# Layer 0 of a two-layer kernel: which matrix products are cut into smaller ones

## The chip, the cores and the metric

The kernel runs on one core of a Trainium2 chip. The metric is the device time of one execution in microseconds (us); less is better. A core has five engines with a queue each: TensorE (PE) multiplies matrices, VectorE (DVE), ScalarE (ACT) and GpSimd (POOL) work on elements, and SyncE (SP) issues most of the transfers between the off-chip memory and the on-chip memory. PE reads its operands from on-chip memory and writes into PSUM, eight banks of 512 float32 columns on 128 partitions, from which the other engines take the results. In the profile a PE product shows as weight loads (PEld) and matmul records (PE).

## What is computed

Two images of 128 channels and 256 by 256 pixels pass through two layers, each with a group normalisation ahead and a residual addition behind. Layer 0 is a windowed attention: every window of 8 x 8 pixels has its queries, every enlarged window of 12 x 12 its keys and values, with four heads of 32 channels, a relative position term, and a mask that keeps only some of the pairs.

```python
qkv = einsum('bchw,oc->bohw', gn(x), W_qkv)
q, k, v = split(qkv, 3, axis=1)
q = windows_8x8(q) * SCALE;  k, v = windows_12x12(k), windows_12x12(v)
attn = einsum('bnd,bmd->bnm', q, k)
attn = attn + rel_pos_emb(q, rel_height, rel_width) + FIXED_MASK
attn = softmax(attn, axis=-1)
out = einsum('bnm,bmd->bnd', attn, v)
x = x + einsum('bchw,oc->bohw', out, W_out)          # layer 0

t1 = conv(gn(x), w1)                                  # 5 x 1
t3 = depthwise_conv(t1, w3)                           # 3 x 1
t4 = einsum('nckhw,ckg->nghw', unfold_w3_dil2(gn(x)), w4)
x = x + t4[:, None] * t3                              # layer 1
```

Everything is float32.

## The kernel before

The mask lets a pixel attend only to pixels of certain row and column parities, so layer 0 is sorted by parity. An image is cut into 32 strips of 8 rows, 64 strips for both (index `k`). A strip is worked off in two units, one for each row parity `r`; unit `u` is `2 * k + r`, and there are 128. Layer 1 follows, strip by strip; its first pieces are called in the last units.

The order of the work is written out by hand in the loop over the units, and each engine keeps to it. For PE a unit has these steps, in this order; the line is that of the matmul in the profile:

1. `biases(u)` (L593): the position coefficients times a constant of ones and zeros are added up in the four score banks `f_s`; 16 products of 32 rows, 64 weight columns and 256 moving columns.
2. `scores(u, split)` (L610): 64 products of keys and queries, added to the same banks. Weights are 64 keys on 64 rows, the moving operand 64 queries: `[2, 32]`, of which the first index is the head of a pair. They go in turn to four quarters of PE's array of 64 rows by 64 columns (`g` picks the rows, `c` the columns). The first `split` of them are made as two products of 32 columns each, with the same weights.
3. `keys(u + 1, cuts, cuts)` (L413, through `in_parts`): two banks `f_pk` of 512 columns, one for each column parity, with the 128 x 128 key weights. `cuts` gives the parts of a bank.
4. `coefficients(k + 1, r)` (L504): one bank `f_pa` with 16 products. The weights `wb` are 128 rows by 64 columns (the position vectors for one place in the window), the moving operand `xq` has 64 columns. `half` decides on which 64 of the bank's partitions, that is on which columns of PE's array, the product lands; the loop runs over eight places `t` and inside it over the two halves. ACT (L513) and DVE (L517) then copy the bank into `f_cf`, one after the other, for the biases of the next strip.
5. `attend(u)` (L636): 64 products of 32 weight columns with 66 moving columns, after ACT has taken the exponentials of the scores (L620, four instructions).
6. In even units `values(k + 1)` (L526), 16 products; in odd units `queries` for the next two units (L476 and L478), 24 products.
7. `project(u)` (L413 again, in the two banks `f_py`), after DVE has divided and transposed the attention's output; DVE adds the residual (L672) and SP stores the rows.

How often a product is cut is set by `pieces(u)`: the parts of a bank for keys, queries and projection, and as a fourth number the scores to be split. `ONE`, `TWO` and `THREE` are the cuts in sixteenths of a bank: `(0, 16)`, `(0, 8, 16)` and `(0, 6, 11, 16)`, so that three parts of a bank have 192, 160 and 160 columns and two have 256 each. Units 0, 1, 60, 62, 63, 64 and 70 have entries of their own in `PIECES`; all others take the default of L316. No values are changed by a cut: the same columns are multiplied, in more or fewer instructions.

A product of float32 operands appears in the trace as two matmul records and two weight loads. All PSUM banks other than the scores' come from one pool of four, taken in turn.

Of the kernel before, what the change touches and what calls it, by code (L numbers as in the profile page):

```python
# [28 lines left out]
ONE, TWO, THREE, FOUR = (0, 16), (0, 8, 16), (0, 6, 11, 16), (0, 4, 8, 12, 16)  # L29
NKEY = 60  # L30
PIECES = {
    0: (ONE, ONE, ONE, 0), 1: (ONE, ONE, THREE, 1),
    60: (THREE, TWO, THREE, 0), 62: (ONE, TWO, ONE, 1), 63: (THREE, TWO, THREE, 3), 64: (TWO, TWO, THREE, 1),
    70: (TWO, TWO, THREE, 1),
}
# [161 lines left out]
def attention_fast(tc, io, x1_d, norm, st_x, st_y, tags, ends, weights, both, layer1):  # L197

    nc = tc.nc
    x = io["x"]  # L200
# [3 lines left out]
    with ExitStack() as l0:  # L204
# [3 lines left out]
        def cload(name, src, shape, pool=cst):  # L208
# [20 lines left out]
        kt = [cst.tile([P, 2, NPAIR * NKEY + 4], F32, tag=f"f_kt{r}", name=f"f_kt{r}") for r in range(2)]  # L229
# [3 lines left out]
        sc = [  # L233
            [ps_s.tile([P, 8, 2, 32], F32, tag=f"s{2 * g + i}", name=f"f_s{g}{i}") for i in range(2)]
            for g in range(2)
        ]

        xq = both.sb.tile([P, 2, 4, 4, 2, 2, 8, 2], F32, tag="xq", name="f_xq")
        wb = both.sb.tile([P, 4, 4, HEADS, 16], F32, tag="wb", name="f_wb")
# [8 lines left out]
        raws, norms, qs, cfs, pts, ots, rcs, ons, x1s = ({} for _ in range(9))  # L248
# [11 lines left out]
        with ExitStack() as setup:  # L260
# [9 lines left out]
            for i in range(first):  # L270
                t = sp.tile([P, 8, W], F32, tag="sx", name=f"f_sx_0_{i}")
                for lo in range(0, 8, 8 if i else 4):
                    hi = lo + (8 if i else 4)
# [28 lines left out]
            for i in range(first, NS - 2):  # L302
                t = sp.tile([P, 8, W], F32, tag="sx", name=f"f_sx_0_{i}")
# [9 lines left out]

        def pieces(u):

            return PIECES.get(u, (THREE, TWO, THREE, 5 if u % 2 else 2 if u % 6 == 0 else 1))  # L316

# [2 lines left out]
        for b in range(NB - 1):  # L322
            row = 0
            for i in range(NS - 4):
                n = 10 if i < 16 else 8
# [20 lines left out]
        def input_stats(u):  # L346
            b, row, n = stats_at[u]
            norm.chunk(st_x[b], row // 2, sxs.pop(u))

        def slots_of(k):  # L350

            first = (4 * k + 2) % 6
            return [(0, 4, first)] if first < 4 else [(0, 2, 4), (2, 2, 0)]
# [135 lines left out]

            return [lambda c=c: part(c) for c in range(2)]  # L490

        def coefficients(k, r):

            if r == 0:
                cfs[k] = wk.tile([P, 2, 2, 2, 8, 2, 16], F32, tag="cf", name=f"f_cf_{k}")
            pa = ps_pj.tile([P, 512], F32, tag="pj", name=f"f_pa_{k}_{r}")  # L500
            for t in range(8):
                t2, t1 = 2 * r + t // 4, t % 4
                for half in range(2):
                    nc.tensor.matmul(  # L504
                        pa[64 * half : 64 * half + 64, 64 * t : 64 * t + 64],
                        wb[:, t2, t1].rearrange("p h x -> p (h x)"),
                        xq[:, half, t2, t1].rearrange("p r c n e -> p (r c n e)"), start=True, stop=True,
                    )
            src = pa.rearrange("p (t m e) -> p e m t", t=8, e=2)
            for i in range(2):  # L510
                dst = cfs[k][..., i, 8 * r : 8 * r + 8].rearrange("p e r c n t -> p e (r c n) t")
                if i == 0:
                    nc.scalar.activation(  # L513
                        dst, src, AF.Identity, bias=keep[:, 1:2], scale=keep[:, 0:1]
                    )
                else:
                    nc.vector.tensor_scalar(  # L517
                        dst, src, keep[:, 2:3], keep[:, 3:4], ALU.mult, ALU.add
                    )
# [79 lines left out]
                                start=e == 0, stop=False, skip_group_check=True,  # L599
                            )  # L600

        def scores(u, split):
            k, r = divmod(u, 2)
            done = 0
            for n in range(NPAIR):
                for g in range(2):
                    rows = slice(64 * g, 64 * g + 64)
                    for c in range(2):
                        for lo, hi in ((0, 1), (1, 2)) if done < split else ((0, 2),):
                            nc.tensor.matmul(  # L610
                                sc[g][n // 8][64 * c : 64 * c + 64, n % 8, lo:hi].rearrange("p i x -> p (i x)"),
                                kt[r][rows, c, NKEY * n : NKEY * n + 64],
                                qs[u][rows, c, n, lo:hi].rearrange("p i x -> p (i x)"),
                                start=False, stop=n % 8 == 7, skip_group_check=True,
                            )
                        done += 1
            pts[u] = wk.tile([P, 2, NPAIR, 2, 32], F32, tag="p", name=f"f_p_{u}", bufs=1)
            for half in range(2):
                for g in range(2):
                    seen["exp", half, g] = nc.scalar.activation(  # L620
                        pts[u][:, g, 8 * half : 8 * half + 8].rearrange("p n i x -> p (n i x)"),
                        sc[g][half].rearrange("p n i x -> p (n i x)"), AF.Exp,
                    )
# [62 lines left out]
        def step():  # L686
            if chains and next(chains[0], True):
                chains.pop()

        def emit(parts):  # L690
            for f in parts:
                f()

        weights.load()
        with tc.manual_schedule(engines=ORDERED):
            normalise(0)
            emit(keys(0, ONE, ONE))
            top_values(0)
            bring_top(0, 0)
            values(0, range(4))  # L700
            for r in range(2):
                bring(r, slots_of(0))
            by_place(0, (0, 4))
            coefficients(0, 0)
            coefficients(0, 1)
            normalise(1)
            by_place(1, (0, 2))
            for u in range(2):
                emit(queries(u, ONE, ONE))
            for u in range(NU):  # L710
                k, r = divmod(u, 2)
                b, s = divmod(k, NS)
                later, more = u + 1 < NU, k + 1 < NB * NS
                if r == 1 and k + 2 < NB * NS:
                    normalise(k + 2)
                if u in stats_at:
                    input_stats(u)
                if u in norm_at:
                    st, i, name = norm_at[u]
                    chains.append(norm.steps(st[i], ps_pj, name, last=False))  # L720
                if u == 8:
                    weights.sums()
                if u in (NU - 4, NU - 2, NU - 1):
                    next(layer1)
                biases(u)
                scores(u, pieces(u)[3])
                if r == 0:
                    if k + 2 < NB * NS:
                        load_rows(k + 2, seen["exp", 0, 0])
                    if s == 0:  # L730
                        bring_top(1, b)
                step()
                at_top = more and (k + 1) % NS == 0
                cuts = pieces(u)[0]
                if later:
                    emit(keys(u + 1, cuts, cuts))
                step()
                if more:
                    coefficients(k + 1, r)
                elif later:  # L740
                    next(layer1)
                if k % NS == NS - 2:
                    step()
                attend(u)
                if u == 2 or u in stats_at:
                    load_next()
                if more and r == 1:
                    bring(1, slots_of(k + 1))
                if not later:
                    next(layer1)  # L750
                turn(u)
                if k % NS == NS - 2:
                    step()
                if r == 0 and more:
                    if at_top:
                        top_values(b + 1)
                        bring_top(0, b + 1)
                    values(k + 1, range(4))
                    bring(0, slots_of(k + 1))
                elif later and more:  # L760
                    cuts = pieces(u)[1]
                    emit(queries(u + 1, cuts, cuts) + queries(u + 2, cuts, cuts))
                if more and r == 0:
                    by_place(k + 1, (2, 4))
                elif k + 2 < NB * NS:
                    by_place(k + 2, (0, 2))
                if u > 0:
                    result_stats(u - 1)
                project(u)
                if u in quarter_at:  # L770
                    st, i, name, part = quarter_at[u]
                    norm.quarter(st[i], name, part)
                del qs[u]
            result_stats(NU - 1)
# [968 lines left out]
```

## Time and profile before

| | |
|---|---|
| median of 3 runs | 2866.58 us (2865.91 to 2869.38) |
| the profiled execution | 2865.81 us, its span 2863.9 us |
| keys, L413 f_pk, records of 160 and 192 columns | 976 and 488, mean 299 and 352 ns |
| projection, L413 f_py, records of 160 and 192 columns | 1008 and 504, mean 299 and 327 ns |
| scores, L610, records of 64 and 32 columns | 15592 and 1584, mean 220 and 223 ns |
| coefficients, L504, records of 64 columns | 4096, mean 225 ns |
| attention, L636 | 16384, mean 220 ns |
| values, L526 | 2048, mean 278 ns |

A record's duration holds the time from its start to a modelled end, and records overlap: the next one has mostly started before one ends, and several run beside each other where they use different parts of the array. So the durations say little on cost; the distance between starts does. A step's cost is read as the time from its first record's start to the first start of the next step. Layer 0 is the stretch from about 113 us to about 1870 us of the span.

### The profile page before, as it was taken

The numbers are of one execution on the slowest core, as the hardware profiler recorded it, in microseconds if no ns is written. First come the engines' busy times: TensorE is split into PE (matmuls) and PEld (weight loads), VectorE is DVE, ScalarE is ACT, GpSimd is POOL, SyncE is SP. The second block draws the span as 40 slices with busy tenths as digits, with TensorE's granted clock in tenths as the row PEclk, the third lists the DMA queues.
The fourth block names the chain that finished last, engine by engine and source line by source line (L and its number), as shares of the span: only waits on it lengthen the run. The fifth ranks groups of instructions, "written<-read, shape, count | busy, mean of one in ns | idle before, by whom it ended". The sixth has DMA issues, their size and how long they took to land.

```text
span 2863.9 us, 117440 instructions
## 1 busy us (share of the span) xinstructions
PE 2749.8 (96%) x51762; PEld 2086.8 (73%) x51762; DVE 2133.8 (75%) x3601; ACT 1506.7 (53%) x2379; POOL 642.8 (22%) x2049
## 2 busy tenths in 40 slices
PE   0699999999999999999999999999999999999998
PEld 0499999999999898999999999854444444444444
DVE  8667777767777565666666666689999998999987
ACT  1345455454554545455454454556666656666654
POOL 1333333333333333333333333200000000000000
PEclk9999999999999999999999999999999999999999
DMA  9566666666666455555554455467888888888885
GB/s 397 169 194 175 193 187 177 195 177 176 184 163 172 120 149 148 129 139 136 146 142 129 140 140 141 122 178 211 225 213 216 218 219 206 221 222 211 216 217 149
DMA packets 157556, 519.74 MB, mean 181 GB/s; under 512 B 20752, under 2 KB 98032, under 8 KB 117232
## 3 DMA queue, kind: packets, MB, share of 16 engines
q1 hardware_dynamic: 147968, 446.07, 52.7%
q0 software_dynamic: 9072, 66.06, 12.4%
q8 instruction: 412, 6.75, 1.0%
q14 instruction: 104, 0.85, 0.1%
HBM read 282.68 MB, written 134.22 MB: 146 GB/s over the span
## 4 chain that ended last, share of the span: by engine, by line
PE 79%; issue 17%; DMA 1%; POOL 1%; ACT 1%; DVE 1%; SPq 0%; POOLq 0%; ACTq 0%; DVEq 0%
PE f_s L610 10%; PE f_o L636 9%; PE f_pk L413 8%; PE f_pv L526 8%; PE f_py L413 8%; PE a_o L923 6%; PE a_e L923 6%; PE f_pq L478 6%; PE f_pa L504 5%; PE f_s L593 5%; PE f_pq L476 2%; PE a_d L974 2%; PE a_c L923 1%; PE b L1016 1%; PE g L903 1%
## 5 line engine op out<-in xcount | busy, mean ns | idle before, releaser
L517 DVE TENSOR_SCALAR f_cf<-f_pa,f_keep 128x512 f32<-128x512 f32 x128 | 103.8, 811 | 539.7 <-ACT f_cf L513 539.6
L620 ACT ACTIVATE f_p<-f_s 128x512 f32<-128x512 f32 x512 | 264.4, 602 | 400.4 <-PE f_s L610 400.3
L484 ACT ACTIVATE f_q<-f_pq,f_head 128x512 f32<-128x512 f32 x512 | 303.4, 703 | 141.0 <-PE f_pq L478 140.9
L427 POOL COPY f_kt<-f_kt 128x60 f32<-128x60 f32 (+1 forms) x348 | 106.2, 341 | 1167.4 <-ACT f_kt L441 1143.7
L998 ACT ACTIVATE t<-t,w 128x1024 f32<-128x1024 f32 x127 | 145.8, 1148 | 367.5 <-DVE t L991 362.5
L404 POOL COPY f_xq<-f_xn 128x96 f32<-128x96 f32 x1024 | 334.3, 356 | 3.3 <-DVE f_xn L387 3.3
L1005 DVE SCALAR_TENSOR_TENSOR t<-t,w,t 128x1024 f32<-128x1024 f32 x254 | 326.0, 1283 | 7.3 <-ACT t L998 1.3
L610 PEld LDWEIGHTS f_s<-f_q,f_kt 64*64 64x64 f32 x17176 | 270.3, 132 | 49.2 <-issue 49.2
L610 PE MATMUL f_s<-f_q,f_kt 64*64 64x64 f32 (+1 forms) x17176 | 287.9, 220 | 0.0
L636 PE MATMUL f_o<-f_vt,f_p 128*32 128x66 f32 x16384 | 263.2, 220 | 1.9 <-issue 1.9
L1034 POOL DMA_DIRECT2D y<-f_x x63 | 54.7, 868 | 916.8 <-DVE y L1026 870.8
L413 PE MATMUL f_pk<-f_xn,f_wqkvT 128*128 128x192 f32 (+3 forms) x1496 | 257.6, 321 | 0.7 <-ACT f_kt L441 0.7
L636 PEld LDWEIGHTS f_o<-f_vt,f_p 128*32 128x32 f32 x16384 | 241.6, 108 | 11.2 <-issue 2.2
L526 PE MATMUL f_pv<-f_wqkvT,f_xn 128*128 128x128 f32 x2048 | 246.2, 278 | 0.8 <-DVE f_cf L517 0.3
L923 PE MATMUL a_o<-xm,w1s 128*128 128x512 f32 x512 | 242.1, 594 | 4.6 <-ACT t L914 4.6
L413 PE MATMUL f_py<-f_ot,f_woT 128*128 128x160 f32 (+1 forms) x1520 | 243.9, 310 | 2.1 <-DVE f_ot L656 1.8
L923 PE MATMUL a_e<-xm,w1s 128*128 128x512 f32 x512 | 240.7, 591 | 0.0
L526 PEld LDWEIGHTS f_pv<-f_wqkvT,f_xn 128*128 128x128 f32 x2048 | 233.8, 192 | 7.2 <-issue 0.8
L413 PEld LDWEIGHTS f_pk<-f_xn,f_wqkvT 128*128 128x128 f32 x1496 | 221.4, 190 | 12.5 <-issue 1.7
L413 PEld LDWEIGHTS f_py<-f_ot,f_woT 128*128 128x128 f32 x1520 | 227.4, 190 | 4.1 <-issue 3.3
L478 PE MATMUL f_pq<-f_xn,f_wq_s 128*128 128x192 f32 (+1 forms) x1008 | 208.9, 329 | 0.0
L645 DVE TENSOR_TENSOR f_on<-f_o,f_rc 128x320 f32<-128x320 f32 (+1 forms) x384 | 197.2, 514 | 13.3
(150 smaller groups left out, 4656.5 us busy)
## 6 DMA issues: line engine op xcount, KB each, us to landing
f_raw<-in_x SPq DMA_DIRECT2D x62, 1280.0 KB
f_x<-f_x SPq DMA_DIRECT2D x128, 512.0 KB
y<-f_x POOLq DMA_DIRECT2D x63, 1024.0 KB, 7.9
out<-y SPq DMA_DIRECT2D x63, 1024.0 KB
f_vt<-f_vn SPq DMA_DIRECT2D x172, 264.0 KB
f_sx<-in_x SPq DMA_DIRECT2D x41, 1024.0 KB
raw<-f_x SPq DMA_DIRECT2D x64, 640.0 KB
raw<-f_x SPq DMA_DIRECT2D x62, 384.0 KB
```

Source lines behind the costliest of these rows:

```text
L404: nc.gpsimd.tensor_copy(xq[:, half, t2, 1:4, :, c].rearrange("p t r n e -> p r t n e"), xn[k % 2][:, windows, :, c, 0:3, t2:8:4].rearrange ...
L413: nc.tensor.matmul(dst[:, 512 * lo // last : 512 * hi // last], w, moving[:, n * lo // last : n * hi // last], start=True, stop=True,)
L478: nc.tensor.matmul(by_pair[:, lo:hi, 8:32], wq_s, xn[k % 2][:, lo:hi, r, c, 0:3].rearrange("p n i j -> p n (i j)"), start=True, stop=True,)
L484: nc.scalar.activation(q[:, c, :, i].rearrange("p n (j t) -> p n j t", t=4), pq.rearrange("p (n t j) -> p n j t", n=NPAIR, t=4), AF.Copy, ...
L526: nc.tensor.matmul(pv[:, P * n : P * n + P], xn[k % 2][:, 4 * g + n].rearrange("p r c i j -> p (r c i j)"), wvT, start=True, stop=True,)
L610: nc.tensor.matmul(sc[g][n // 8][64 * c : 64 * c + 64, n % 8, lo:hi].rearrange("p i x -> p (i x)"), kt[r][rows, c, NKEY * n : NKEY * n + 6 ...
L620: seen["exp", half, g] = nc.scalar.activation(pts[u][:, g, 8 * half : 8 * half + 8].rearrange("p n i x -> p (n i x)"), sc[g][half].rearran ...
L636: nc.tensor.matmul(po[32 * h : 32 * h + 32, n - lo], p[:, h // 2, n, h % 2], vt[r][:, :, n, h], start=True, stop=True,)
L645: nc.vector.tensor_tensor(on[:, :, lo:hi].rearrange("p c n d -> p n c d"), po[:, :, :, 0:32], rc.to_broadcast([P, hi - lo, 2, 32]), ALU.mult,)
L923: nc.tensor.matmul(pa[:, : n * W], w, rows, start=i == 0, stop=i == len(terms) - 1)
L998: nc.scalar.activation(t3[:, j : j + 4], t1[:, j : j + 4, :], AF.Copy, scale=w3[:, 0:1])
L1005: nc.vector.scalar_tensor_tensor(t3[:, j : j + 4], t1[:, j + tap : j + tap + 4, :], w3[:, tap : tap + 1], t3[:, j : j + 4], ALU.mult, ALU.add,
```

## The change

The default of `pieces` cuts keys and projection into two parts a bank, and the fourth number is larger. `scores` loses its argument: all its products are whole. `coefficients` gets one: of the 16 products of its bank, the first `split` are made as two products of 32 moving columns, with the same weights each time. The loop hands it the fourth number of `pieces`. The table `PIECES` stays as it is, so its fourth numbers now count coefficient products too.

```diff
-            return PIECES.get(u, (THREE, TWO, THREE, 5 if u % 2 else 2 if u % 6 == 0 else 1))
+            return PIECES.get(u, (TWO, TWO, TWO, 9 if u % 2 else 6 if u % 6 == 0 else 5))
...
-        def coefficients(k, r):
+        def coefficients(k, r, split=0):
...
                 for half in range(2):
-                    nc.tensor.matmul(
-                        pa[64 * half : 64 * half + 64, 64 * t : 64 * t + 64],
-                        wb[:, t2, t1].rearrange("p h x -> p (h x)"),
-                        xq[:, half, t2, t1].rearrange("p r c n e -> p (r c n e)"), start=True, stop=True,
-                    )
+                    for lo, hi in ((0, 1), (1, 2)) if 2 * t + half < split else ((0, 2),):
+                        nc.tensor.matmul(
+                            pa[64 * half : 64 * half + 64, 64 * t + 32 * lo : 64 * t + 32 * hi],
+                            wb[:, t2, t1].rearrange("p h x -> p (h x)"),
+                            xq[:, half, t2, t1, lo:hi].rearrange("p r c n e -> p (r c n e)"),
+                            start=True, stop=True,
+                        )
...
-        def scores(u, split):
+        def scores(u):
             k, r = divmod(u, 2)
-            done = 0
...
-                        for lo, hi in ((0, 1), (1, 2)) if done < split else ((0, 2),):
-                            nc.tensor.matmul(
-                                sc[g][n // 8][64 * c : 64 * c + 64, n % 8, lo:hi].rearrange("p i x -> p (i x)"),
-                                kt[r][rows, c, NKEY * n : NKEY * n + 64],
-                                qs[u][rows, c, n, lo:hi].rearrange("p i x -> p (i x)"),
-                                start=False, stop=n % 8 == 7, skip_group_check=True,
-                            )
-                        done += 1
+                        nc.tensor.matmul(
+                            sc[g][n // 8][64 * c : 64 * c + 64, n % 8].rearrange("p i x -> p (i x)"),
+                            kt[r][rows, c, NKEY * n : NKEY * n + 64],
+                            qs[u][rows, c, n].rearrange("p i x -> p (i x)"),
+                            start=False, stop=n % 8 == 7, skip_group_check=True,
+                        )
...
-                scores(u, pieces(u)[3])
+                scores(u)
...
-                    coefficients(k + 1, r)
+                    coefficients(k + 1, r, pieces(u)[3])
```

## The prediction

> **What bounds the kernel now.** I read the busy shares first, then the waits of TensorE, then the stretch of layer 0 by engine, then two neighbouring units (one unit is half a strip of 8 rows) in order of time. The page's first part and the chain by engine and line:
>
> ```profile
> PE 2749.8 (96%) x51762; PEld 2086.8 (73%) x51762; DVE 2133.8 (75%) x3601; ACT 1506.7 (53%) x2379; POOL 642.8 (22%) x2049
> PE 79%; issue 17%; DMA 1%; POOL 1%; ACT 1%; DVE 1%; SPq 0%; POOLq 0%; ACTq 0%; DVEq 0%
> PE   0699999999999999999999999999999999999998
> PEclk9999999999999999999999999999999999999999
> ```
>
> TensorE (PE) is the bound on average, at full clock. The change touches layer 0 alone, so its own stretch counts. The stage table for two long stretches of it (columns: stretch, its length, then busy time and instructions of PE, its weight loads, DVE, ACT and POOL, clock, DMA share and rate):
>
> ```profile
> 200.00:939.00 739.00, 738.66 (x20385) 683.15 (x20375) 528.95 (x1078) 373.23 (x684) 241.54 (x826) 1.00 0.65 180
> 1110.00:1848.00 738.00, 737.45 (x20413) 681.22 (x20412) 449.07 (x945) 373.30 (x684) 235.08 (x809) 1.00 0.53 138
> ```
>
> PE is idle 0.3 us in 739, and the next engine, DVE, works 529. What lengthens or shortens PE's work here goes straight into the time. Units 50 (even) and 51 (odd) in order of time (start, length to the last end, line, operation, shape of the first, number of records):
>
> ```profile
> 802.01 1.12 PE L593 MATMUL f_s<-f_cf,f_hot 32*64 32x256 f32 x32
> 803.06 2.19 PE L610 MATMUL f_s<-f_q,f_kt 64*64 64x32 f32 x130
> 805.18 2.00 PE L413 MATMUL f_pk<-f_xn,f_wqkvT 128*128 128x192 f32 x12
> 807.12 1.15 PE L504 MATMUL f_pa<-f_xq,f_wb 128*64 128x64 f32 x32
> 808.20 2.05 PE L636 MATMUL f_o<-f_vt,f_p 128*32 128x66 f32 x128
> 810.18 3.84 PE L526 MATMUL f_pv<-f_wqkvT,f_xn 128*128 128x128 f32 x32
> 813.85 1.90 PE L413 MATMUL f_py<-f_ot,f_woT 128*128 128x192 f32 x12
> 815.68 1.12 PE L593 MATMUL f_s<-f_cf,f_hot 32*64 32x256 f32 x32
> 816.73 2.31 PE L610 MATMUL f_s<-f_q,f_kt 64*64 64x32 f32 x138
> 818.97 2.00 PE L413 MATMUL f_pk<-f_xn,f_wqkvT 128*128 128x192 f32 x12
> 820.90 1.15 PE L504 MATMUL f_pa<-f_xq,f_wb 128*64 128x64 f32 x32
> 821.99 2.05 PE L636 MATMUL f_o<-f_vt,f_p 128*32 128x66 f32 x128
> ```
>
> The reader is to subtract starts. A product is two records (128 for 64 whole score products, 32 for 16 coefficient products), and each split product adds two. A step costs from its start to the next one's: scores 2.12 us with one split (unit 50) and 2.24 with five (unit 51), keys 1.94, coefficients 1.08, projection 1.83. The same row with none, two and three splits, from units 60, 54 and 63, each with the step that follows it:
>
> ```profile
> 940.24 2.10 PE L610 MATMUL f_s<-f_q,f_kt 64*64 64x64 f32 x128
> 942.27 0.38 PE L161 MATMUL pv_x<-q_x,f_gavg 128*128 128x1 f32 x2
> ...
> 857.84 2.21 PE L610 MATMUL f_s<-f_q,f_kt 64*64 64x32 f32 x132
> 859.98 0.73 PE L413 MATMUL f_pk<-f_xn,f_wqkvT 128*128 128x192 f32 x3
> ...
> 983.81 2.22 PE L610 MATMUL f_s<-f_q,f_kt 64*64 64x32 f32 x134
> 985.96 1.13 PE L453 MATMUL f_pk_top<-f_top,f_wqkvT 128*128 128x256 f32 x4
> ```
>
> So 0, 1, 2, 3 and 5 splits cost 2.03, 2.12, 2.14, 2.15 and 2.24 us. The cost isn't linear: the first costs 0.09 to 0.10, the second and third 0.01 each, and the fifth brings it to 0.21. That is the key to the change. The score products go in turn to four 64x64 quarters of the array, which work beside each other. The first split puts one quarter behind by two records; the next three are in the other quarters and lie beside it; the fifth is again in the first. What counts is the number of splits in the fullest quarter: n of them cost about 117n - 20 ns.
>
> **What the skill says.** "TensorE: Matmul & The Clock Gate", section "LDWEIGHTS (loading the stationary operand)", gives a weight load as columns / 1.2 ns, whatever the rows: 53 ns for 64 columns. "TensorEngine Tiling (Array Packing)", "Key Properties", says that tiles load and multiply in parallel, and its "Instruction Overhead" warns that a matmul with few moving columns is no shorter than one with 60. The trace agrees: within a quarter, score records start 58 ns apart, for 64 moving columns as for 32. A 32-column record saves nothing, since the 64 columns of weights are loaded again for it: 2 x 58 = 117 ns, the slope found above. "Runtime: NRT & Kernel Launch", "Instruction fetch mechanics", says that instructions arrive in blocks of 256; the page's q8 row (412 packets, 6.75 MB, so 16 KB each) fits that. It bears on a rival below.
>
> **The change part by part.** By `pieces`, an odd unit now has nine split coefficient products where it had five split score products; an even one five (six in every sixth unit) where it had one (two). Keys and projection go from three parts a bank to two. The products of a unit stay 189 (190 in every sixth): -2 keys, -2 projection, -5 or -1 or -2 scores, +9 or +5 or +6 coefficients. With "k+1 exists" and the table PIECES, 61 odd units, 39 plain even and 19 sixth ones are concerned; units 0, 1, 60, 62, 63, 64 and 70 swap nothing or equal numbers.
>
> *Scores removed.* Odd 2.24 - 2.03 = 0.21 us; even 0.10; sixth 0.11.
>
> *Keys and projection.* Between records of 160, 192 and 256 columns the trace has 136, 162 and 216 ns. Three parts in two banks: 8 x 136 + 4 x 162 = 1736 ns; two parts: 8 x 216 = 1728. So 8 ns less for each, 16 a unit: next to nothing, since columns and not instructions set this cost. The keys' second record is 105 ns late after the switch from the scores (267 instead of 162); that switch stays.
>
> *Coefficients added.* They use two column halves of the array with 64 weight columns each, records again 58 ns apart in a half (16 x 58 = 0.93, with 0.15 of start the 1.08 seen). The splits go to t = 0, 1, ... and there to half 0, then half 1. Nine: five in half 0, four in half 1. Five: three and two. Six: three each. No row shows a 32-column coefficient product. From below it costs what its columns cost, half as much, so almost nothing; from above the two halves get in each other's way and each split takes 175 ns. I take the score's law, for the weights have the same 64 columns and the records the same 58 ns: 5 x 117 - 20 = 565 ns for nine, 3 x 117 - 20 = 331 for five, 337 for six (a few ns of later start).
>
> *Sum.* Odd: +565 - 213 - 16 = +336 ns, x61 = 20.5 us. Plain even: +331 - 97 - 16 = +218, x39 = 8.5. Sixth: +337 - 110 - 16 = +211, x19 = 4.0. Unit 63 (three splits, two in half 0): +0.1. Units 126 and 127 have no coefficients left to make and lose 0.35. Together +32.8 us. The profiled execution took 2865.81 us (span 2863.9), 0.8 below the median of 2866.58; on the median the sum is 2899.4. I forecast 2899.
>
> *What hides or follows.* Nothing hides it: PE is not waiting. What waits for the coefficients (ACT's and DVE's f_cf, L513 and L517, then DVE's reciprocals and transposes for the projection) runs from their end, and the attention and value or query products that cover it follow at the same distance. The exponentials on ACT (4 x 0.60 us after the scores) get more cover, not less. No DMA, SP or POOL instruction is moved and no wait is added. Layer 1 starts that much later and is as long as before.
>
> **Rivals.**
>
> *A 32-column coefficient record is bound by its columns.* Then the removed parts win: odd -229, even -113, sixth -126 ns, in all -20.8 us; with 5 ns for each added record in the fuller half (50 and 30 ns a unit) +4.8 us come back: 2851. For it speaks only that this shape isn't in the trace with all 128 rows; against it the 58 ns of the 32-column score records with the same weight width. It decides if a split costs less than 117n - 20 by about 60%. Chance 0.06.
>
> *The halves no longer run side by side.* Four records in one half before the other's first: 175 ns a split, +129 us, about 2996. The scores with five splits show quarters starting 13 ns apart and running together, so 0.03.
>
> *Block boundaries of the instruction stream.* A unit is 378 records with as many weight loads and some twelve waits, 768 instructions or three blocks, so a boundary keeps its place in the unit. Before the attention, the new order moves products against it by up to 28 instructions. If a boundary then opened a gap of the size of the exposed weight load (105 ns) in each unit, +12.5 us on top: 2912. No such gap is seen before. Chance 0.06.
>
> *The change doesn't reach the end*, as other engines were late anyway: the 0.3 us of idle in 739 leaves no room; 0.01 for about no change.
>
> **The numbers.** Forecast 0.84, column-bound 0.06, serial halves 0.03, boundaries 0.06, no effect 0.01. The forecast's own bounds: records 53 ns apart (the load alone) give +27, no saving at the start +37. Range 2892 to 2907: it leaves out the column-bound, serial and boundary cases, 0.15 together. A measurement of this kernel can tell a change from none above about 0.2%, 5.7 us. Faster 0.06, same 0.01, slower 0.93.
>
> **What will show it.** Scores at 2.03 us in all units; coefficients at 1.65 us (odd) and 1.41 (even); keys and projection shorter by 0.01 each; an odd unit 13.71 to 14.04, an even one 13.67 or 13.69 to about 13.90; f_pa's records 4096 to 5826, f_s at L610 from 17176 to 16384; the gap between records of a half 58 ns at 32 columns too. A coefficient step under 1.3 us in odd units would make the forecast wrong, and so would a new idle place of PE.

## The result and the profile after

The changed kernel takes 2900.49 us (median of 4 runs, 2897.63 to 2902.3) against 2867.24 for the kernel before: ratio 1.0113, 95% interval 1.0101 to 1.0125. It is 33 us slower, where 2899 us was forecast. Its profiled execution took 2902.3 us, with a span of 2900.4.

The page of the changed kernel, busy shares and chain, and the stage table for a stretch of layer 0 (columns as before):

```profile
PE 2785.0 (96%) x51736; PEld 2046.2 (71%) x51736; DVE 2132.9 (74%) x3601; ACT 1507.3 (52%) x2379; POOL 641.6 (22%) x2049
PE 80%; issue 17%; DMA 1%; POOL 1%; DVE 1%; ACT 0%; SPq 0%; POOLq 0%; DVEq 0%; ACTq 0%
```

```profile
200.00:950.00 750.00, 748.75 (x20293) 659.13 (x20296) 523.81 (x1066) 369.06 (x677) 238.19 (x816) 1.00 0.63 177
```

PE executes 26 records fewer than before and is busy 35 us longer. It is nearly as closely packed as it was (idle 1.3 us of these 750, where it was 0.3 of 739), so the time is in the records, not between them. One plain even unit and the odd one after it, in order of time:

```profile
818.15 2.10 PE L610 MATMUL f_s<-f_q,f_kt 64*64 64x64 f32 x128
820.17 2.00 PE L413 MATMUL f_pk<-f_xn,f_wqkvT 128*128 128x256 f32 x8
822.10 1.50 PE L505 MATMUL f_pa<-f_xq,f_wb 128*64 128x32 f32 x42
823.52 2.05 PE L635 MATMUL f_o<-f_vt,f_p 128*32 128x66 f32 x128
825.50 3.84 PE L528 MATMUL f_pv<-f_wqkvT,f_xn 128*128 128x128 f32 x32
829.17 1.89 PE L413 MATMUL f_py<-f_ot,f_woT 128*128 128x256 f32 x8
831.00 1.12 PE L595 MATMUL f_s<-f_cf,f_hot 32*64 32x256 f32 x32
832.04 2.10 PE L610 MATMUL f_s<-f_q,f_kt 64*64 64x64 f32 x128
834.07 1.99 PE L413 MATMUL f_pk<-f_xn,f_wqkvT 128*128 128x256 f32 x8
835.99 1.73 PE L505 MATMUL f_pa<-f_xq,f_wb 128*64 128x32 f32 x50
837.65 2.05 PE L635 MATMUL f_o<-f_vt,f_p 128*32 128x66 f32 x128
```

Start to start, the scores are down to 2.03 us in both, keys and projection are 1.93 and 1.83 (shorter by 0.01), and the coefficients went from 1.08 to 1.42 (five splits) and 1.66 us (nine). The typical (median) step over all units, from its start to the next step's start in nanoseconds (a sixth unit is an even one whose number six divides, a plain even one is any other):

| step | before | after | forecast of the difference | measured |
|---|---|---|---|---|
| scores, odd / plain even / sixth | 2238 / 2122 / 2135 | 2025 | -213 / -97 / -110 | -213 / -97 / -110 |
| keys and projection, each | 1934, 1830 | 1924, 1820 | -8 | -10 |
| coefficients, odd (nine splits) | 1082 | 1658 | +565 | +576 |
| coefficients, plain even (five) | 1082 | 1419 | +331 | +337 |
| coefficients, sixth (six) | 1082 | 1451 | +337 | +369 |

With 61, 39 and 19 units the measured column gives 20.9 + 8.6 + 4.5 us, with the special and last units 33.8. The medians differ by 33.25.

### The profile page after: what moved, and what is told of

It reads as the page before. It is cut to its first block, busy times and chain, and to the rows that moved or that the text cites. A ratio compares the mean times of both kernels' runs of the same rounds, so it can differ in the third digit from the quotient of the medians.

```text
span 2900.4 us, 117389 instructions
## 1 busy us (share of the span) xinstructions
PE 2785.0 (96%) x51736; PEld 2046.2 (71%) x51736; DVE 2132.9 (74%) x3601; ACT 1507.3 (52%) x2379; POOL 641.6 (22%) x2049
## 4 chain that ended last, share of the span: by engine, by line
PE 80%; issue 17%; DMA 1%; POOL 1%; DVE 1%; ACT 0%; SPq 0%; POOLq 0%; DVEq 0%; ACTq 0%
PE f_s L610 9%; PE f_o L635 9%; PE f_pk L413 9%; PE f_pv L528 8%; PE f_py L413 8%; PE f_pa L505 7%; PE a_o L922 6%; PE a_e L922 6%; PE f_pq L478 6%; PE f_s L595 5%; PE f_pq L476 2%; PE a_d L973 2%; PE a_c L922 1%; PE b L1015 1%; PE g L902 1%
## 5 line engine op out<-in xcount | busy, mean ns | idle before, releaser
L610 PEld LDWEIGHTS f_s<-f_q,f_kt 64*64 64x64 f32 x16384 | 250.7, 135 | 49.5 <-issue 49.5
L610 PE MATMUL f_s<-f_q,f_kt 64*64 64x64 f32 x16384 | 268.4, 220 | 0.2 <-issue 0.2
L413 PE MATMUL f_pk<-f_xn,f_wqkvT 128*128 128x256 f32 (+2 forms) x1016 | 256.5, 395 | 0.7 <-ACT f_kt L441 0.7
L413 PE MATMUL f_py<-f_ot,f_woT 128*128 128x256 f32 (+3 forms) x1036 | 242.4, 377 | 2.0 <-DVE f_ot L655 1.8
L505 PEld LDWEIGHTS f_pa<-f_xq,f_wb 128*64 128x64 f32 x5826 | 186.2, 137 | 44.5 <-issue 43.5
L505 PE MATMUL f_pa<-f_xq,f_wb 128*64 128x32 f32 (+1 forms) x5826 | 203.7, 225 | 1.5 <-ACT f_kt L441 0.8
```

Source lines behind the costliest of these rows:

```text
L413: nc.tensor.matmul(dst[:, 512 * lo // last : 512 * hi // last], w, moving[:, n * lo // last : n * hi // last], start=True, stop=True,)
L505: nc.tensor.matmul(pa[64 * half : 64 * half + 64, 64 * t + 32 * lo : 64 * t + 32 * hi], wb[:, t2, t1].rearrange("p h x -> p (h x)"), xq[:, ...
L610: nc.tensor.matmul(sc[g][n // 8][64 * c : 64 * c + 64, n % 8].rearrange("p i x -> p (i x)"), kt[r][rows, c, NKEY * n : NKEY * n + 64], qs[ ...
```

## The experiments

A ratio below is to the kernel before on the same chip, whose medians lay between 2867.3 and 2869.2 us. Two questions were left: whether the place of a split, and not the number of splits, is what costs; and why the number of products in a unit was the same before and after.

**Splits of one half first.** The changed kernel, with one line different: the splits fill half 0 of the array's columns before they start on half 1.

```diff
-                    for lo, hi in ((0, 1), (1, 2)) if 2 * t + half < split else ((0, 2),):
+                    for lo, hi in ((0, 1), (1, 2)) if 8 * half + t < split else ((0, 2),):
```

> The changed kernel with as many split coefficient products, but in the order of halves: all eight places of half 0 first, then half 1. Equal instructions and columns in all. Theory, the fullest half counts (117 n - 8 ns): odd units 8 in half 0, coefficients 1.08 + 0.93 = 2.01 us; even 5, 1.66; sixth 6, 1.78. Against the changed kernel 61 x 352 + 39 x 240 + 19 x 325 ns = +37 us: about 2937 us. Rival, each added instruction has its own price wherever it lands: no change from 2900 us.

Measured: 2936.4 us, ratio 1.0238 (1.0221 to 1.0255). Its odd coefficient step, with the 50 records of the changed kernel:

```profile
821.06 2.05 PE L505 MATMUL f_pa<-f_xq,f_wb 128*64 128x32 f32 x50
823.04 2.05 PE L635 MATMUL f_o<-f_vt,f_p 128*32 128x66 f32 x128
```

1.98 us instead of 1.66, for the same instructions; five took 1.65 and six 1.78. The price of a split depends on which half it lands in: the fullest half sets the step. Five splits in half 0 and none in half 1 take 1.65 us here, five and four took 1.66 in the changed kernel, so the four lie beside the five. The rival, a fixed price for each instruction, falls.

**Splits in the attention.** The kernel before with whole scores and as many splits in the attention's products, whose weights have 32 columns.

```diff
-                scores(u, pieces(u)[3])
+                scores(u, 0)
...
-                attend(u)
+                attend(u, pieces(u)[3])
...
-                        nc.tensor.matmul(
-                            po[32 * h : 32 * h + 32, n - lo], p[:, h // 2, n, h % 2],
-                            vt[r][:, :, n, h], start=True, stop=True,
-                        )
+                        for c0, c1 in ((0, 1), (1, 2)) if 4 * n + h < split else ((0, 2),):
+                            nc.tensor.matmul(
+                                po[32 * h : 32 * h + 32, n - lo, c0:c1], p[:, h // 2, n, h % 2],
+                                vt[r][:, c0:c1, n, h], start=True, stop=True,
+                            )
```

> The kernel before with as many splits (5, 2 or 1), moved from the scores to the attention's products, whose weights have 32 columns instead of 64 (66 moving columns become two times 33). The instruction count of a unit is that of before. Theory, a record lasts as long as the longer of its weight columns and its moving columns: at 32 weight and 33 moving columns that is about 32 ns instead of 58, so two in place of one cost 0 to 25 ns a unit; with the whole scores 19.7 us less and 1 to 2 us more: about 2849 us. Rival, each added pair of records costs some 40 ns whatever its weights: about 2867 us as before.

Measured: 2855.45 us, ratio 0.9957 (0.9941 to 0.9974). An odd unit's attention with five splits:

```profile
817.54 2.10 PE L637 MATMUL f_o<-f_vt,f_p 128*32 128x33 f32 x138
819.57 0.49 PE L476 MATMUL f_pq<-f_xn,f_wq_s 128*128 128x128 f32 x2
```

2.03 us here and 2.01 in most units, against 1.98 whole: some 35 ns for five splits, 7 for one, where the same splits cost the scores 213 and 97. So here, with narrower weights, a split is nearly free. The expected 2849 us is missed by 6; PE has small gaps in the value products here (64 steps with a mean of 3725 ns and a median of 3675, 3.2 us in all).

**The changed kernel with its splits in the attention.** Same cuts, same nine, six or five splits, coefficients whole:

```diff
-                    coefficients(k + 1, r, pieces(u)[3])
+                    coefficients(k + 1, r)
...
-                attend(u)
+                attend(u, pieces(u)[3])
```

> The changed kernel with its 9, 6 or 5 splits in the attention's products in place of the coefficients'; cuts, counts and boundaries as in the changed kernel. Theory, place decides: the coefficient steps fall back to 1.08 us (-55.3 us), the attention gains 7 ns for each split (61 x 63 + 19 x 42 + 39 x 35 ns = +6.0): about 2851 us, up to 2855 with small gaps. Rival, the changed kernel is slow for the number of its splits (9 against 5): 2890 us or more.

Measured: 2860.09 us (20 runs, 2855.46 to 2868.17), ratio 0.9971 (0.9964 to 0.9978). Coefficients and attention of an odd unit:

```profile
792.44 1.15 PE L505 MATMUL f_pa<-f_xq,f_wb 128*64 128x64 f32 x32
793.53 2.27 PE L636 MATMUL f_o<-f_vt,f_p 128*32 128x33 f32 x146
795.73 0.49 PE L476 MATMUL f_pq<-f_xn,f_wq_s 128*128 128x128 f32 x2
```

The coefficients are back at 1.08 us, and 40 us of the changed kernel's time are gone with them, of 49 expected. This is the clean trial of the change's costly part, since nothing else differs in the code. Two things were off. Nine splits cost 130 ns (typical step 2107 against 1977), not 63: up to six a split costs 7 ns, and why nine cost more stays open. And PE has small gaps here too, 3.7 us in the value products and some 3 in the attention.

**Whole scores and nothing in their place.** One line of the kernel before: `scores(u, 0)`.

> The kernel before with every score product whole (no split, nothing in its place; 1 to 5 products fewer a unit). Theory, TensorE's work sets the time and a split costs what its fullest quarter of the array takes: scores 2.03 us in every unit, 61 x 213 + 39 x 97 + 19 x 110 ns and 0.8 us for the special units and the last two, in all 19.7 us less: about 2847.5 us. Rival, the block boundaries of the instruction stream: the splits held a unit at three blocks of 256 instructions; without them the boundaries wander through all steps, PE shows new gaps, and the gain is at least half eaten: 2857 us or more.

Measured: 3025.84 us, ratio 1.055 (1.0532 to 1.0567): not 20 us faster but 158 slower, with less work. TensorE's waits (who waited for what, us in total, times, longest) and one even unit in order of time:

```profile
PE f_o L636 <- issue: 100.8, 55, 3.9
...
PE f_s L610 <- issue: 10.3, 12, 1.5
```

```profile
325.16 1.15 PE L504 MATMUL f_pa<-f_xq,f_wb 128*64 128x64 f32 x32
326.24 1.80 PE L636 MATMUL f_o<-f_vt,f_p 128*32 128x66 f32 x107
330.37 0.54 PE L636 MATMUL f_o<-f_vt,f_p 128*32 128x66 f32 x21 [2.33 <-issue]
330.84 1.38 PE L526 MATMUL f_pv<-f_wqkvT,f_xn 128*128 128x128 f32 x10
```

PE stands still for 2.33 us in the middle of the attention, and waits for nothing that the profile shows. The gaps come and go. Units 21 to 27 take 13.50 us (odd) and 13.58 (even), the time that TensorE's work predicts; units 28 to 37 take 14.5 to 19.8 us; 41 to 45 are good again. From one even unit to the next the gap in the attention moves on by 12 to 14 records (units 28 to 36). A unit has now about 756 instructions, 12 short of three blocks of 256, and the 24 of two units are 12 records: the gap walks with the block boundary. (In these counts an odd unit's queries are 12 products, 24 records, and not the 24 products of the list of steps.) The good units are those whose first instruction stands between about place 162 and 217 of 256, counted from PE's first instruction in the trace, with small gaps up to 250. The kernel before keeps its units between 212 and 234.

**Only the boundaries moved.** The kernel before with its score splits; in one unit, 32 attention products become 64 (with the edit of `attend` above).

```diff
-                attend(u)
+                attend(u, 32 if u == 2 else 0)
```

> The kernel before, whole score splits and all, with 32 products of one attention (unit 2) made as two, once. Every later unit has the instructions of before; only the block boundaries of the instruction stream stand 131 instructions elsewhere in it. Theory, where the boundaries stand decides: in the run with whole scores the units whose start stood so in its block were longer by about 4.6 us (even) and 1.15 us (odd), so 62 x 5.77 = +358 us: about 3225 us, 3140 at least. Rival, not the place of the boundaries but the number of products in a unit made the run with whole scores slow: only the 32 products count, at 7 ns each: 2868 us.

Measured: 3188.44 us, ratio 1.1115 (1.1095 to 1.1135). TensorE's waits and one even unit:

```profile
PE f_o L637 <- issue: 211.5, 119, 4.5
...
PE f_pk L413 <- issue: 9.3, 26, 0.6
```

```profile
643.25 1.15 PE L504 MATMUL f_pa<-f_xq,f_wb 128*64 128x64 f32 x32
644.33 1.57 PE L637 MATMUL f_o<-f_vt,f_p 128*32 128x66 f32 x93
648.50 0.77 PE L637 MATMUL f_o<-f_vt,f_p 128*32 128x66 f32 x35 [2.60 <-issue]
649.20 3.84 PE L526 MATMUL f_pv<-f_wqkvT,f_xn 128*128 128x128 f32 x32
```

The gap is in nearly every unit, around record 83 to 103 of the attention. From unit 3 on the instructions of a unit are those of the kernel before; nothing but their place in the stream changed. (By the trace they stand 127 places further on, 128 instructions more and one semaphore wait fewer, and not 131.) This settles it: the place of the boundaries is worth over 300 us, and the number of products only matters because it moves them.

The traces say the same without any forecast. Number PE's instructions from the first (weight loads, matmul records, semaphore waits). In this run, the one with whole scores and the next two, 326 times over 0.6 us pass between two starts of PE from 150 to 1850 us of the span, and 316 of these stops stand at place 192 or 193 of 256. The trace's transfers of instructions (the q8 queue, 16384 bytes each) fit: in 56 of the 65 gaps of over 1.2 us (between two starts, from 150 to 2000 us of the span) such a packet starts in the gap or at most 0.5 us ahead of it, and PE resumes 1.37 us (median) after the packet's end. That PE waits for it is read from this order; no view names it.

The stops are not the whole of the 319 us. Behind some of them PE's granted clock is halved for a while. A value step under it, between the attention and the projection:

```profile
253.82 0.77 PE L637 MATMUL f_o<-f_vt,f_p 128*32 128x66 f32 x37 [3.14 <-issue]
254.52 5.47 PE L526 MATMUL f_pv<-f_wqkvT,f_xn 128*128 128x128 f32 x32
259.83 1.90 PE L413 MATMUL f_py<-f_ot,f_woT 128*128 128x192 f32 x12
```

It takes 5.31 us instead of 3.68, and the granted clock from 254 to 260 us is 0.72 in the mean. This trace has 35 stretches at half clock in layer 0, most of 3.4 us, 126 us in all; the run with whole scores has 20 (72 us), and the kernel before none. Each begins in a stop of over 1.6 us between two starts, or at most 1.5 us after it. At half speed they cost about 63 and 36 us, an estimate from their lengths. So some stops of PE are paid twice here.

**The coefficient splits alone.** The kernel before with the new `coefficients` and its 9, 6 or 5 splits, scores and cuts as they were.

> The kernel before plus the coefficient splits alone (9, 6 or 5), with the score splits and the three parts kept. Theory: the coefficient steps are those of the changed kernel (1.66, 1.45 and 1.42 us against 1.08), 61 x 576 + 19 x 369 + 39 x 337 ns = +55.3 us: about 2922.5 us. Rival, longer coefficients are partly covered or partly paid by what else the change did: clearly less than +50 us. A unit has 5 to 9 products more here, so boundaries of the instruction stream wander; if they cost, it is more than +58 us.

Measured: 3131.04 us, ratio 1.0919 (1.0883 to 1.0956). The typical coefficient steps are 1.66, 1.45 and 1.43 us as in the changed kernel, so the 55 us are there, and about 208 us came on top: 117.6 us of waits of the attention for "issue", 16.4 in the scores, and 21 stretches at half clock (75 us). A unit has 20 to 36 instructions over three blocks here.

**Two parts alone.** One line of the kernel before:

```diff
-            return PIECES.get(u, (THREE, TWO, THREE, 5 if u % 2 else 2 if u % 6 == 0 else 1))
+            return PIECES.get(u, (TWO, TWO, TWO, 5 if u % 2 else 2 if u % 6 == 0 else 1))
```

> The kernel before with two parts a bank for keys and projection, and nothing in place of the four products that this takes from each unit. By TensorE's work alone, 119 x 20 ns = 2.4 us less: 2865 us. Theory: a unit now has 752 instructions, so the block boundaries move by 16 a unit through all steps; weighed with what the units of the runs with whole scores and with the coefficients alone lost at each place of the boundary (183 and 198 us over all units), about 2867.5 - 2.4 + 190 = 3055 us, 3020 to 3090. Rival, only the particular places of those two runs were costly: 2865 to 2950 us.

Measured: 3048.12 us, ratio 1.0627 (1.0603 to 1.0652). What the units of two other runs lost at each place of the boundary foretold this one within 7 us. A cut that saves 2.4 us of work costs 180 by itself.

**Boundaries 24 instructions back, splits in the attention.** On top of the attention splits:

```diff
-    0: (ONE, ONE, ONE, 0), 1: (ONE, ONE, THREE, 1),
+    0: (ONE, ONE, ONE, 0), 1: (ONE, ONE, ONE, 0), 2: (THREE, TWO, THREE, 0),
```

> The kernel with the splits in the attention, and the key and projection cuts and splits of units 1 and 2 made fewer, so that all later boundaries stand 24 instructions further back in the unit. Theory: the small gaps that PE still shows there in the value products (about 3.2 us in all) and once in the scores (0.5) go, as the units in that place of the block had none in the run with whole scores: about 2851 us. Rival, these gaps come from other engines or transfers: 2855 us as with the splits in the attention alone.

Measured: 2850.42 us (5 runs, 2846.45 to 2856.38), ratio 0.9935 (0.9922 to 0.9949). The value steps are now 3673 ns in the mean, so their gaps are gone, but others came: 1.0 us in the scores of unit 65 and 1.8 in the attention of unit 74. The interval overlaps that of the attention splits alone, so the gain of the shift isn't shown by the times. All three versions with the splits in the attention beat both kernels, by 0.3 to 0.7% against the kernel before.

**The same for the changed kernel.** `1: (ONE, ONE, ONE, 0), 2: (TWO, TWO, TWO, 4)` in its table.

> The changed kernel with the boundaries of all units from 3 on standing 24 instructions further back (fewer cuts and splits in units 1 and 2). Theory: the gaps in the value products, 2.9 us over the changed kernel's trace, go; the coefficient steps stay: about 2897 us. Rival, more of the changed kernel's loss than this lies in the boundaries: clearly below 2895 us.

Measured: 2901.47 us, ratio 1.0118 (1.01 to 1.0135), no better than the changed kernel. The gaps in the value products went (mean 3673 ns against 3720, 3.0 us), but others came that it hadn't, 2.8 us once in a projection (unit 64) and 0.6 in the scores of unit 64 among them. The gaps left at a good place are of the size of what separates two executions, and this shift gains nothing sure. The loss of 33 us stays, so it doesn't lie in the boundaries.

## Why the prediction was right

*PE is the only bound in layer 0.* It held: the difference of PE's own steps, 33.8 us, is within 1 us the difference of the medians, and no wait came or went by more than 3 us.

*The scores' law carried over to the coefficients.* This was the step with no row of its own, taken from the scores' 117n - 20 for the fullest part of the array. That line was drawn through two points, one and two splits in a quarter, and used here for three and five. Measured, nine and five splits cost 576 and 337 ns against 565 and 331. The term for six was too small, 369 against 337: with three in each half, half 1 probably ends later than half 0, which I had put at a few ns, while with unequal halves that is covered; the trace doesn't name the halves, so this isn't shown. It makes 0.6 us. With the splits of one half first, the law's other side was tried, and the same instructions cost 36 us more, where 37 were forecast. The records of the coefficients show the 58 ns too: with 32 moving columns they mostly start 58 to 59 ns apart within a half.

*A record is as long as its weight columns or its moving columns ask, whichever is more.* This was the reason given for the law, with the Trainium skill's price of a weight load ("TensorE: Matmul & The Clock Gate", "LDWEIGHTS (loading the stationary operand)"). The attention trial agrees: with 32 weight columns instead of 64 a split costs 7 ns (14 where there are nine) instead of over 50. Weights and position in the unit differ there together, so the reason is supported and not isolated.

*Keys and projection gain next to nothing.* 10 ns each, forecast 8.

*The bounds.* One of the two doesn't come out of its own terms: without the saving of 20 ns at the start, 119 units take 2.4 us more, which makes +35 us and not +37. Nothing rests on it.

*The rivals.* Column-bound coefficients and serial halves are refuted by the coefficient steps. The boundary rival was right in kind and wrong in size. I named the three blocks of a unit and priced a badly placed boundary at 105 ns, the largest exposed load that the trace showed; the runs show up to 7 us for one unit (20.8 us for unit 28 with the boundaries moved, 13.7 before). It did no harm to the forecast because the change moves the boundaries by at most 28 instructions within a unit and not from unit to unit; the three runs that change the number of products in a unit, by one to nine, missed the sum of TensorE's own work by 178 to 209 us. That the places the change moves to are as good as the old ones was luck, as nothing in the profile before told good places from bad. The value products' gaps, 1.1 us before and 2.9 us in the changed kernel's trace, are probably what the shift within the unit did.

## What to carry to other kernels

Here small products that share PE's array were priced by the fullest part of it and, as far as shown, by the wider of weights and moving operand, so try cuts where the weights are narrow, and spread them evenly. Where PE runs without a gap through very short instructions, the place of the block boundary can cost more than the work: keep the count of a repeated stretch at a whole number of blocks, and test a change of PE's instructions with the count kept. The count alone is not enough: with the boundaries moved it is kept, and each unit meets the same bad place, which made the slowest run of all. When less work makes such a kernel slower, look for waits on "issue" that walk through the loop, and for a lower granted clock behind them.

## What was not expected of the hardware

The Trainium skill ("Runtime: NRT & Kernel Launch", "Instruction fetch mechanics") calls the crossing of a block boundary mostly hidden. Here it is hidden only at some places. In the attention, 256 instructions run in 1.98 us, and a boundary at its later records stopped PE for 0.2 to 4.5 us; at other places of the same loop it cost nothing. Moving the same instructions by 127 places in the stream made the kernel 11% slower. Why the next block comes too late there isn't shown. That its instructions are short is not enough: with the boundaries moved, 82 of the 97 blocks that PE ran through in under 3 us (between 200 and 1850 us of the span) ended in a stop of over 0.5 us, but with the splits in the attention and the boundaries 24 instructions back only 1 of 82 such blocks did.
